# Two non-local attention blocks on one core: chunks of 512 pixels, keys spread over four batches, and the weights W prepared in steps

## The chip, the cores and the metric

The kernel runs on one core of one Trainium2 chip. Its engines are named as in the profile: PE (TensorE, matrix multiplication), DVE (VectorE), ACT (ScalarE), POOL (GpSimd) and SP (SyncE, which here starts most DMAs). The metric is the device time of one execution in microseconds (us). The profile shows one execution of its own. Its span, from the first to the last instruction, is a little shorter than its device time.

## What is computed

Two layers of the same form are applied in turn to `x` of shape (4, 128, 96, 96) in float32: four images of 9216 pixels with 128 channels. One layer, cut to what matters:

```python
g_x = maxpool2(conv1x1(x, g_w, g_b))          # 64 channels, 48 x 48 keys
theta_x = conv1x1(x, theta_w, theta_b)        # 64 channels, 9216 queries
phi_x = maxpool2(conv1x1(x, phi_w, phi_b))    # 64 channels, 48 x 48 keys
attn = softmax(theta_x^T phi_x)               # 9216 x 2304 for each image
y = attn g_x
W_y = conv1x1(y, W_w, W_b), then batch norm with stored mean and variance
return W_y + x
```

The pooling takes the largest of every 2 x 2 pixels, so one image has 2304 keys, in 18 tiles of 128. The order of the keys is free, as long as phi and g have the same.

## The kernel before, in words

**Blocks.** A block is one layer of one image. `ORDER` lists the eight blocks so that a block's predecessor in the same image lies at least one block back. The keys of a block are made while the block ahead of it is at work; only the first block's keys have to be made at the start. After the main program, `general_blocks` would be run if a check of the sums of exponentials failed. That code is not touched.

**Pairs and batches.** A pair is 1024 pixels (two tiles of 512); a block has nine, the program 72. For each pair the 18 key tiles are taken two at a time in nine batches, 648 in all, counted by `t` in one long loop. In each batch PE makes the scores of two key tiles (`scores`, L312), ACT takes their exponential with a constant shift in place of the maximum (L318), DVE adds the results up (`add_up`, L325 and L327), and PE multiplies the batch before by the values (`values`, L335). A matmul uses a 64 x 64 quarter of the array, and four run side by side. Each float32 matmul stands in the trace as two instructions.

**Cycles and slots.** Eighteen batches, two pairs, are a cycle. The slot `s` is the place in it. The other work is put into slots by hand:

- the two thetas for a later pair (`thetas`, slots 5 and 6),
- the sums of the two pairs that are done (`denominators`, slot 3, from the tile `folded`),
- `inverses`, `normalise`, and the projection with W (`multiply`, then `add`, slots 8 and 11),
- the chunks for the next block's keys (`chunks`, slots from `CHUNK_SLOTS` = 1, 13, 15, 17, the first half in one batch and the second half in the next).

All of these use the two PSUM banks of the pool `ps_misc`. Scores have two double banks of their own (`ps_sc`), and the exponentials have seven buffers (`EXPS`).

**The order of the queues is that of the program text.** In a batch it is: scores of the first tile, the `first` piece of other work, scores of the second tile, the `second` piece; then DVE's adds with `take` (the reading of the banks) after the first of them; then the values of the batch before; then the small DVE work, and last the spreads and the list `after`. Each engine executes its own part of this in order.

**Keys.** A chunk is 384 pixels, four rows of the image. PE makes g (partitions 0 to 63) and phi (64 to 127), DVE takes the maximum of 2 x 2 (`pool`, L224) into `gphi`. There are 24 chunks in a block, two at a time. When eight chunks are there (six key tiles), two batches later `spread` does in one go: for the first six tiles the centre, the mean of phi over them (L251, L252); phi less the centre on ACT (L253) and its copy to the other 64 partitions (L256); and eight DVE transposes of g, 32 x 192 each (L264), into `gT`.

**The first block.** It has spreads of three tiles (`FIRST_GT`). Eight chunks and two spreads come ahead of batch 0, and four chunks each in batches 0, 1, 3 and 4 (`between`), with the spreads named in `after`.

**W.** `make_scale`, `make_W` (a PE transpose at L109 and two DVE copies) and `make_shift` (a matmul with W at L161 and DVE work) run one right after another: for layer 0 after batch 7, for layer 1 after batch 18.

Of the kernel before, what the change touches and what calls it, by code (L numbers as in the profile page):

```python
# [9 lines left out]
F32 = mybir.dt.float32  # L10
# [6 lines left out]
P = 128  # L17
B, C, CI, H, W = 4, 128, 64, 96, 96
HW = H * W
# [16 lines left out]
NB = NKT // KB  # L36
EXPS = 7
FIRST_GT = 3
WARM = (5, 3)
CYCLE = 2 * NB  # L40
CHUNK_SLOTS = (1, 13, 15, 17)
# [6 lines left out]
def shifted_blocks(ctx: ExitStack, tc: tile.TileContext, x: bass.AP, layers, out: bass.AP, flag):  # L48
# [58 lines left out]
    def transposed(src, rows, cols, name, twice=False):  # L107
        ps = ps_misc.tile([P, QT], F32, tag="misc", name=f"{name}_ps")
        nc.tensor.transpose(ps[:cols, :rows], src, ident[:rows, :rows])  # L109
        t = const.tile([2 * cols if twice else cols, rows], F32, name=name)  # L110
        nc.vector.tensor_copy(t[:cols, :], ps[:cols, :rows])
        if twice:
            nc.vector.tensor_copy(t[cols:, :], ps[:cols, :rows])
        return t
# [58 lines left out]
    def columns(wanted, name, engine):  # L173

        rows = prep.tile([len(wanted), C], F32, name=f"rows_{name}")
        for i, (w, key) in enumerate(wanted):
            n = w.p[key].shape[0]
            for h in range(C // n):
                engine.dma_start(out=rows[i : i + 1, ts(h, n)], in_=as_row(w.p[key]))

        def make():
            cols = transposed(rows, len(wanted), C, f"cols_{name}")
            for i, (w, key) in enumerate(wanted):
                w.col[key] = cols[:, i : i + 1]

        return make
# [15 lines left out]
    class Block:  # L202
# [5 lines left out]
        def begin_keys(self, gt):  # L208
            name, self.gt = self.name, gt
            self.gphi = kvp.tile([P, NK], F32, tag="gphi", name=f"gphi_{name}", bufs=1)  # L210
            self.phi = kvp.tile([P, NK], F32, tag="phi", name=f"phi_{name}")
            self.gT = kvp.tile([P, NKT, CI], F32, tag="gT", name=f"gT_{name}")
            self.centre = kvp.tile([P, 1], F32, tag="centre", name=f"centre_{name}")

        def products(self, r, ps):

            for h in range(2):
                nc.tensor.matmul(
                    ps[ts(h, CI), :CC], lhsT=self.w.gphi[:, ts(h, CI)],
                    rhs=self.xt[:, ts(r, CC)], start=True, stop=True,  # L220
                )

        def pool(self, r, ps):
            nc.vector.tensor_reduce(  # L224
                self.gphi[:, ts(r, CC // 4)].rearrange("p (h w) -> p h w", w=W // 2),
                ps[:, :CC].rearrange("p (h a w b) -> p h w a b", a=2, b=2, w=W // 2),
                AX.XY,
                ALU.max,
            )

        def pooled(self, r):

            ps = ps_misc.tile([P, QT], F32, tag="misc", name=f"gphi_ps_{self.name}_{r}")
            self.products(r, ps)
            self.pool(r, ps)

        def pooled_2(self, r):

            ps = ps_sc.tile([P, PT], F32, tag="sc", name=f"gphi_ps_{self.name}_{r}")
            for step in (self.products, self.pool):  # L240
                for c in range(2):
                    step(r + c, ps[:, ts(c, QT)])

        def spread_phi(self, i):

            gphi, phi, centre, n = self.gphi, self.phi, self.centre, self.gt * KT
            keys = ts(i, n)
            if i == 0:  # L250
                nc.vector.tensor_reduce(centre[CI:, :], gphi[CI:, keys], AX.X, ALU.add)  # L251
                nc.vector.tensor_scalar(centre[CI:, :], centre[CI:, :], -1.0 / n, None, ALU.mult)  # L252
            nc.scalar.activation(  # L253
                phi[CI:, keys], gphi[CI:, keys], AF.Identity, bias=centre[CI:, :]
            )
            nc.scalar.copy(phi[:CI, keys], phi[CI:, keys])  # L256

        def spread_g(self, i):

            tiles = ts(i, self.gt)  # L260
            g = self.gphi[:CI, :].rearrange("p (t k) -> p t k", k=KT)
            for k in range(KT // 32):
                for c in range(CI // 32):
                    nc.vector.transpose(  # L264
                        self.gT[ts(k, 32), tiles, ts(c, 32)], g[ts(c, 32), tiles, ts(k, 32)]
                    )

        def spread(self, i):
            self.spread_phi(i)
            self.spread_g(i)  # L270

        def chunks(self, r):

            pss = two_banks(f"gphi_ps_{self.name}_{r}")

            def part(i, rows, c):
                return (
                    pss[i][ts(c, CI), :CC], self.w.gphi[rows, ts(c, CI)],
                    self.xt[rows, ts(r + i, CC)],
                )  # L280

            def take():
                for i in range(2):
                    self.pool(r + i, pss[i])

            return crosswise(part, take)

# [206 lines left out]
    def begin(n, gt=GT):  # L494

        blocks[n].xt = xs[ORDER[n][0]]
        blocks[n].begin_keys(gt)
# [12 lines left out]
    begin(0, FIRST_GT)  # L510
# [6 lines left out]
    b0.pooled(1)  # L517
    first_cols()
    for w in ws:
        w.make_std()  # L520
    nc.scalar.preload_act_table(AF.Exp)
    b0.pooled_2(2)
    th = ps_sc.tile([P, PT], F32, tag="sc", name="theta_ps_0")[:, :QT]
    pairs[0].theta(th)
    pairs[0].take_theta(th)
    b0.spread_phi(0)
    b0.pooled(4)
    b0.pooled(5)
    b0.pooled_2(6)
    b0.spread_phi(1)  # L530
    b0.spread_g(0)
    xs[1] = load_x(1)
    between = {0: 8, 1: 12, 3: 16, 4: 20}
    after = {
        0: [lambda: b0.spread_g(1)],
        1: [lambda: b0.spread_phi(2), lambda: b0.spread_g(2)],
        2: [lambda: b0.spread_phi(3), lambda: b0.spread_g(3)],
        4: [lambda: b0.spread_phi(4), lambda: b0.spread_g(4)],
        5: [lambda: b0.spread_phi(5), lambda: b0.spread_g(5)],
        6: [other_cols, ws[0].make_scale, ws[1].make_scale],  # L540
        7: [ws[0].make_W, ws[0].make_shift],
        NB: [ws[1].make_gphi, ws[1].make_theta],
        2 * NB: [ws[1].make_W, ws[1].make_shift],
# [3 lines left out]
    for n in range(1, len(blocks)):  # L547
        lo = (n - 1) * NP * NB if n > 1 else CYCLE
        slots = [t for t in range(lo, n * NP * NB - 4) if t % CYCLE in CHUNK_SLOTS]
        items = HW // CC // 2  # L550
        for i in range(items):
            keys[slots[i * (len(slots) - 1) // (items - 1)]] = (n, i)
# [3 lines left out]
    for t in range(total + 1):  # L556
# [4 lines left out]
        if t in keys:  # L561
            n, i = keys[t]
            if i == 0:
                begin(n)
            first, *pending = blocks[n].chunks(2 * i)
            if i % 4 == 3:
                spreads[t + 2] = lambda n=n, i=i: blocks[n].spread(i // 4)
        elif t < total and s == 5:
            if q < late:
                first, *pending = thetas(pairs[q + 1 : q + 3])  # L570
            else:
                ps = ps_misc.tile([P, QT], F32, tag="misc", name="theta_ps_last")
                first, take = (lambda: odd.theta(ps)), (lambda: odd.take_theta(ps))
        elif gone and s == 3:
            second, take = denominators(gone, folded)
        elif gone and s in (8, 11):
            second, take = gone[s // 11].multiply, gone[s // 11].add
# [15 lines left out]
        if second:  # L593
            second()
        for i in range(KB):
# [4 lines left out]
        if t in between:  # L600
            b0.pooled(between[t])
            b0.pooled(between[t] + 1)
            b0.pooled_2(between[t] + 2)
        if gone and s in (9, 12):
            gone[s // 12].note(gone[s // 12].rc)
# [4 lines left out]
        if t < total:  # L610
            if gone:
                one, two = gone
                if s == 1:
                    two.fold(folded)
                    two.add_halves()
                if s in (4, 5):
                    one.inverses(one.rc, ((0, 1), (2, 3))[s - 4])
                if s == 6:
                    one.normalise()
                if s in (6, 7, 8):  # L620
                    two.inverses(two.rc, ((0,), (1, 2), (3,))[s - 6])
                if s == 9:
                    two.normalise()
            if s == 10:
                even.add_halves()
            if s == 12 and q < late:
                even.fold(folded)
            if q == late:
                if s == 10:
# [3 lines left out]
                    even.inverses(even.rc)  # L633
                if s == 13:
                    even.note(even.rc)
                    even.normalise()
                if s == 15:
# [7 lines left out]
        if t in spreads:  # L645
            spreads.pop(t)()
        for step in after.pop(t, []):
            step()
    assert not spreads and not after
# [322 lines left out]
```

## Time and profile before

| what | us |
|---|---|
| device time, median of 3 runs | 2556.34 (2555.39 to 2557.2) |
| device time of the profiled execution | 2556.96 |
| its span | 2554.8 |
| PE busy in the span | 2523.5 (99%) |
| DVE busy | 2144.2 (84%) |
| ACT busy | 1627.2 (64%) |
| DMA, 59.92 MB | 23 GB/s in the mean |
| start of batch 0, first scores | 12.62 |

Such a page is read as follows. A row of instructions has the line in the kernel, the engine, the operation, what is written from what, the shape and the count; behind the first bar the busy time and the mean duration of one in ns; behind the second bar how long the engine was idle just ahead of such instructions, and whose end let it go on. Busy time of PE counts matmuls that overlap, so 99% does not say how fast they follow each other. In a line of the timeline stand the start in us, the time covered, the engine, the line and the operation, with the count of merged instructions and, in brackets, the idle time ahead of it and what ended it. A line of the waits has the engine and what waited, what it waited for, and then the total in us, how often, and the longest. The granted clock is the share of TensorE's full clock that the profile shows, 0.998 over the whole span.

### The profile page before, as it was taken

What the parts mean: (1) busy time and instruction counts of PE and PEld (TensorE: products, weight loads), DVE (VectorE), ACT (ScalarE), POOL (GpSimd) and SP (SyncE); (2) the same over time, 40 slices, a digit from 0 to 9 for tenths busy, and PEclk for the clock granted to TensorE, in tenths of its full rate; (3) what the DMA queues carried; (4) which work ended last, traced back from release to release, by engine and by line L of the source; (5) the groups of instructions that cost most, each with busy time, mean ns of one, the idle gap of its engine ahead of it and who ended that gap; (6) DMA issues with size and microseconds to landing.
All of it is one profiled execution on the core that took longest, in us unless ns stands there. A gap on an engine that the chain in (4) does not pass through costs nothing.

```text
span 2554.8 us, 54104 instructions
## 1 busy us (share of the span) xinstructions
PE 2523.5 (99%) x23650; PEld 1128.0 (44%) x23650; DVE 2144.2 (84%) x2330; ACT 1627.2 (64%) x1786; POOL 0.7 (0%) x6
## 2 busy tenths in 40 slices
PE   9999999999999999999999999999999999999998
PEld 3333566346653333334665333333466533333332
DVE  7778888888888888888888888888888888888888
ACT  5656666666666666666666666666666666666665
POOL 0000000000000000000000000000000000000000
PEclk9999999999999999999999999999999999999999
DMA  4020000000000000020000000000000000000000
GB/s 153 10 83 10 10 5 10 10 9 10 6 9 26 26 26 26 14 83 9 10 10 5 26 26 26 26 18 8 7 10 10 18 26 14 26 26 26 26 26 35
DMA packets 16586, 59.92 MB, mean 23 GB/s; under 512 B 2635, under 2 KB 3541, under 8 KB 16341
## 3 DMA queue, kind: packets, MB, share of 16 engines
q1 hardware_dynamic: 16172, 56.31, 7.2%
q8 instruction: 187, 3.06, 0.5%
q14 instruction: 59, 0.48, 0.1%
q10 hardware_dynamic: 168, 0.07, 0.0%
HBM read 19.14 MB, written 18.87 MB: 15 GB/s over the span
## 4 chain that ended last, share of the span: by engine, by line


## 5 line engine op out<-in xcount | busy, mean ns | idle before, releaser
L318 ACT ACTIVATE exp<-sc,nshift 128x1024 f32<-128x1024 f32 x1296 | 1387.4, 1112 | 850.8 <-PE sc L312 844.4
L327 DVE TENSOR_TENSOR sum<-sum,exp 128x1024 f32<-128x1024 f32 x1151 | 1399.1, 1216 | 332.8 <-ACT exp L318 287.7
L312 PE MATMUL sc<-theta,phi 64*64 64x512 f32 x10368 | 1308.6, 590 | 11.6 <-ACT exp L318 8.4
L335 PE MATMUL av<-exp,gT 64*64 64x512 f32 x10368 | 1275.9, 589 | 0.0
L312 PEld LDWEIGHTS sc<-theta,phi 64*64 64x64 f32 x10368 | 494.0, 133 | 619.3 <-issue 452.4
L335 PEld LDWEIGHTS av<-exp,gT 64*64 64x64 f32 x10368 | 494.0, 133 | 602.5 <-issue 475.3
L355 DVE RECIPROCAL halves<-halves 128x128 f32<-128x128 f32 x280 | 250.8, 927 | 0.0
L198 PE MATMUL gphi_ps<-x,gphiT 64*64 64x384 f32 x1344 | 148.8, 482 | 0.0
L224 DVE TENSOR_REDUCE gphi<-gphi_ps 128x96 f32<-128x384 f32 x192 | 97.4, 550 | 26.6 <-PE gphi_ps L198 23.8
L325 DVE TENSOR_TENSOR sum<-exp,exp 128x1024 f32<-128x1024 f32 x72 | 87.5, 1215 | 32.3 <-ACT exp L318 29.8
L198 PEld LDWEIGHTS gphi_ps<-x,gphiT 64*64 64x64 f32 x1344 | 66.0, 133 | 78.2 <-issue 55.9
L394 DVE SCALAR_TENSOR_TENSOR x<-W_ps,shift,x 128x512 f32<-128x512 f32 x142 | 99.4, 742 | 0.0
L342 ACT COPY halves<-av 128x1024 f32<-128x1024 f32 x71 | 71.9, 1012 | 27.3 <-PE av L335 26.2
L368 DVE TENSOR_TENSOR folded<-folded,sum 64x1024 f32<-64x1024 f32 x70 | 85.1, 1216 | 1.1
L198 PE MATMUL theta_ps<-x,thetaT 64*64 64x512 f32 x560 | 79.2, 589 | 0.0
L385 PE MATMUL W_ps<-halves,WT 64*64 64x512 f32 x568 | 79.1, 589 | 0.0
L264 DVE STREAM_TRANSPOSE gT<-gphi 32x192 f32<-32x192 f32 (+1 forms) x216 | 74.7, 346 | 2.8
L376 DVE TENSOR_TENSOR halves<-halves 128x512 f32<-128x512 f32 x71 | 48.9, 688 | 0.7
L379 DVE TENSOR_TENSOR halves<-halves 128x512 f32<-128x512 f32 x70 | 47.9, 684 | 0.0
L445 PE MATMUL den_ps<-folded,ones 64*64 64x512 f32 x280 | 40.3, 592 | 6.5 <-DVE gphi L224 6.5
L359 ACT ACTIVATE halves<-den_ps 128x512 f32<-128x512 f32 x70 | 41.1, 600 | 7.5 <-PE den_ps L445 7.5
L372 ACT ACTIVATE halves<-halves 128x512 f32<-128x512 f32 x70 | 44.0, 628 | 0.0
(89 smaller groups left out, 265.3 us busy)
## 6 DMA issues: line engine op xcount, KB each, us to landing
folded<-sum SPq DMA_DIRECT2D x70, 256.0 KB
out_dram<-x SPq DMA_DIRECT2D x35, 512.0 KB
x<-in_x_dram SPq DMA_DIRECT2D x18, 768.0 KB
x<-in_x_dram SPq DMA_DIRECT2D x12, 384.0 KB
out_dram<-x SPq DMA_DIRECT2D x4, 128.0 KB
gphi_nat<-in_L_conv_phi_w_dram SPq DMA_DIRECT2D x2, 32.0 KB
rows_other<-in_L_conv_g_b_dram SPq DMA_DIRECT2D x4, 0.2 KB
W_nat<-in_L_conv_W_w_dram SPq DMA_DIRECT2D x2, 32.0 KB
```

Source lines behind the costliest of these rows:

```text
L198: nc.tensor.matmul(out, lhsT=lhsT, rhs=rhs, start=step == 0, stop=step == 1)
L224: nc.vector.tensor_reduce(self.gphi[:, ts(r, CC // 4)].rearrange("p (h w) -> p h w", w=W // 2), ps[:, :CC].rearrange("p (h a w b) -> p h w ...
L264: nc.vector.transpose(self.gT[ts(k, 32), tiles, ts(c, 32)], g[ts(c, 32), tiles, ts(k, 32)])
L312: nc.tensor.matmul(ps[ts(c, CI), ts(h, QT)], lhsT=self.blk.phi[ts(h, CI), ts(2 * k + c, CI)], rhs=self.th[ts(h, CI), :], start=True, stop= ...
L318: nc.scalar.activation(e, ps, AF.Exp, bias=nshift)
L325: nc.vector.tensor_add(self.sum, self.es[0], e)
L327: nc.vector.tensor_add(self.sum, self.sum, e)
L335: nc.tensor.matmul(self.av[ts(h, CI), ts(r, QT)], lhsT=self.blk.gT[ts(r, CI), k, :], rhs=e[ts(r, CI), ts(h, QT)], start=(k == 0), stop=(k ...
L355: nc.vector.reciprocal(self.rc[:, ts(i, P)], src[:, ts(i, P)])
L368: nc.vector.tensor_add(folded[here, :], folded[here, :], self.sum[here, :])
L385: nc.tensor.matmul(self.pss[h][ts(c, CI), :], lhsT=self.blk.w.W[ts(h, CI), ts(c, CI)], rhs=self.y[ts(h, CI), :], start=True, stop=True,)
L394: nc.vector.scalar_tensor_tensor(dst, self.pss[h], self.blk.w.shift, dst, op0=ALU.add, op1=ALU.add)
```

## The change

- A chunk is 512 pixels and gives exactly one tile of 128 keys. A 96-pixel row does not divide so; a chunk is 8 rows of the left 64 columns, or 16 rows of the right 32. A block has 18 chunks, two at a time, nine items. The moving operand of these matmuls is no longer one contiguous stretch but 8 or 16 of them.
- The items stand at batches 15, 17 and 31 of a double cycle of 36, counted on by one cycle (`KEYS`): slots 13, 15 and 17. Slot 1 has none any more.
- The sums move from slot 3 to 2, the second projection from 11 to 12, and the odd pair's `fold` ahead of the batch's adds in slot 1. Inverses come one in each batch, halves of both pairs are added in slot 1.
- A spread of six tiles takes four batches: centre (first spread only), phi and two transposes in the first; the copy of phi and two transposes in the second; two transposes in each of the other two.
- The first block: four chunks ahead of batch 0, then two in each of the batches 0 to 6, two batches ahead of their use by the scores; phi is made for two tiles at a time, the transposes for six tiles in batches 0, 3 and 6. The centre is the mean over two tiles.
- `make_scale`, `make_W`, `make_shift` and the remaining weights for layer 1 come in the batches 10 to 13, a step in each.

The core of the diff:

```diff
+KEYS = (15, 17, 31)
+THETAS, SUMS, PROJECT = 5, 2, (8, 12)
-FIRST_GT = 3
-CHUNK_SLOTS = (1, 13, 15, 17)
...
+        def chunk(self, k, rows):
+            first, height, left, width = ((0, 8, 0, 64), (8, 8, 0, 64), (0, 16, 64, 32))[k % 3]
+            first += k // 3 * 16
+            pixels = self.xt[rows, :].rearrange("p (h w) -> p h w", w=W)
+            return pixels[:, first : first + height, left : left + width]
...
+        def centring(self, n):
+            centre, gphi = self.centre, self.gphi
+            nc.vector.tensor_reduce(centre[CI:, :], gphi[CI:, : n * KT], AX.X, ALU.add)
+            nc.vector.tensor_scalar(
+                centre[CI:, :], centre[CI:, :], -1.0 / (n * KT), None, ALU.mult
+            )
+
+        def centred(self, keys):
+            nc.scalar.activation(
+                self.phi[CI:, keys], self.gphi[CI:, keys], AF.Identity, bias=self.centre[CI:, :]
+            )
+
+        def copied(self, keys):
+            nc.scalar.copy(self.phi[:CI, keys], self.phi[CI:, keys])
+
+        def square(self, i, k):
+            tiles = ts(i, GT)
+            g = self.gphi[:CI, :].rearrange("p (t k) -> p t k", k=KT)
+            for c in range(CI // 32):
+                nc.vector.transpose(
+                    self.gT[ts(k, 32), tiles, ts(c, 32)], g[ts(c, 32), tiles, ts(k, 32)]
+                )
...
+    pairs[0].theta(th)
+    b0.centring(KB)
+    b0.centred(ts(0, KB * KT))
+    b0.copied(ts(0, KB * KT))
+    pairs[0].take_theta(th)
     for w in ws:
         w.make_std()
     nc.scalar.preload_act_table(AF.Exp)
+    b0.pooled(1)
+    b0.centred(ts(1, KB * KT))
+    b0.copied(ts(1, KB * KT))
...
     after = {
+        10: [other_cols, ws[0].make_scale, ws[1].make_gphi, ws[1].make_scale],
+        11: [ws[0].make_W, ws[1].make_W],
+        12: [ws[0].make_shift, ws[1].make_shift],
+        13: [ws[1].make_theta],
     }
...
     for n in range(1, len(blocks)):
+        cycle = (n - 1) * NP * NB // CYCLE * CYCLE
+        for j in range(NB):
+            t = cycle + KEYS[j % len(KEYS)] + j // len(KEYS) * CYCLE
+            keys[t] = (n, j)
+            if j % len(KEYS) == len(KEYS) - 1:
+                spreads[t + 2] = (blocks[n], j // len(KEYS))
...
+        if gone and s == 1:
+            gone[1].fold(folded)
+        if t + 2 < NB:
+            b0.pooled(t + 2)
         for i in range(KB):
             if t < total:
                 pairs[now].add_up(j * KB + i)
             if i == 0 and take:
                 take()
+        if t + 2 < NB:
+            b0.centred(ts(t + 2, KB * KT))
+            b0.copied(ts(t + 2, KB * KT))
+            if t % 3 == 0:
+                for k in range(KT // 32):
+                    b0.square(t // 3, k)
...
+            for i, pair in enumerate(gone):
                 if s == 1:
+                    pair.add_halves()
+                k = s - PROJECT[i] + 5
+                if k in range(QT // P):
+                    pair.inverses(pair.rc, (k,))
+                if k == QT // P - 1:
+                    pair.normalise()
+            if s == 13 and q < late:
                 even.fold(folded)
...
+        for k in range(KT // 32):
+            if t - k in spreads:
+                blk, i = spreads[t - k]
+                if k == 0:
+                    if i == 0:
+                        blk.centring(GT)
+                    blk.centred(ts(i, GT * KT))
+                if k == 1:
+                    blk.copied(ts(i, GT * KT))
+                blk.square(i, k)
```

More of the change, by code (lines that the diff above doesn't have):

```diff
@@ L105, in as_row, with transposed @@
         return src.rearrange("(o c) -> o c", o=1)
-    def transposed(src, rows, cols, name, twice=False):
-        ps = ps_misc.tile([P, QT], F32, tag="misc", name=f"{name}_ps")
+    def transposed(src, rows, cols, name, twice=False, ps=None):
+        if ps is None:
+            ps = ps_misc.tile([P, QT], F32, tag="misc", name=f"{name}_ps")
         nc.tensor.transpose(ps[:cols, :rows], src, ident[:rows, :rows])
@@ L179, in columns, with make @@
                 engine.dma_start(out=rows[i : i + 1, ts(h, n)], in_=as_row(w.p[key]))
-        def make():
-            cols = transposed(rows, len(wanted), C, f"cols_{name}")
+        def make(ps=None):
+            cols = transposed(rows, len(wanted), C, f"cols_{name}", ps=ps)
             for i, (w, key) in enumerate(wanted):
@@ L206, in __init__, with begin_keys @@
             self.xt, self.w, self.store, self.name = xt, w, store, name
-        def begin_keys(self, gt):
-            name, self.gt = self.name, gt
+        def begin_keys(self):
+            name = self.name
             self.gphi = kvp.tile([P, NK], F32, tag="gphi", name=f"gphi_{name}", bufs=1)
@@ L213, in begin_keys, with pool @@
             self.centre = kvp.tile([P, 1], F32, tag="centre", name=f"centre_{name}")
[L215 to L223, printed above, removed]
+        def chunk(self, k, rows):
[3 more added lines that the diff above has]
+            return pixels[:, first : first + height, left : left + width]
+        def pool(self, k, ps):
+            w = self.chunk(k, slice(0, CI)).shape[2] // 2
             nc.vector.tensor_reduce(
-                self.gphi[:, ts(r, CC // 4)].rearrange("p (h w) -> p h w", w=W // 2),
-                ps[:, :CC].rearrange("p (h a w b) -> p h w a b", a=2, b=2, w=W // 2),
+                self.gphi[:, ts(k, KT)].rearrange("p (h w) -> p h w", w=w),
+                ps.rearrange("p (h a w b) -> p h w a b", a=2, b=2, w=w),
                 AX.XY,
@@ L229, in pool @@
             )
[L231 to L240, printed above, removed]
-                for c in range(2):
[L242 to L265, printed above, removed]
-                    )
[L268 to L274, printed above, removed]
+        def pooled(self, j):
+            pss = two_banks(f"gphi_ps_{self.name}_{j}")
+            for i in range(2):
+                rhs = self.chunk(j * KB + i, slice(0, P))
+                for c in range(2):
+                    nc.tensor.matmul(
+                        pss[i][ts(c, CI), :], lhsT=self.w.gphi[:, ts(c, CI)], rhs=rhs,
+                        start=True, stop=True,
+                    )
+            for i in range(2):
+                self.pool(j * KB + i, pss[i])
@@ L276, in part, with chunks @@
+        def chunks(self, j):
+            pss = two_banks(f"gphi_ps_{self.name}_{j}")
             def part(i, rows, c):
                 return (
-                    pss[i][ts(c, CI), :CC], self.w.gphi[rows, ts(c, CI)],
-                    self.xt[rows, ts(r + i, CC)],
+                    pss[i][ts(c, CI), :], self.w.gphi[rows, ts(c, CI)],
+                    self.chunk(j * KB + i, rows),
                 )
@@ L283, in take @@
                 for i in range(2):
-                    self.pool(r + i, pss[i])
+                    self.pool(j * KB + i, pss[i])
             return crosswise(part, take)
+        def centring(self, n):
[17 more added lines that the diff above has]
+                )
     class Pair:
@@ L492, in shifted_blocks, with begin @@
         blocks.append(Block(None, ws[l], store, f"{b}_{l}"))
-    def begin(n, gt=GT):
+    def begin(n):
         blocks[n].xt = xs[ORDER[n][0]]
-        blocks[n].begin_keys(gt)
+        blocks[n].begin_keys()
     pairs = [Pair(blk, p, n * NP + p) for n, blk in enumerate(blocks) for p in range(NP)]
@@ L507, in busy @@
             nc.tensor.matmul(warm[:, :P], lhsT=ident, rhs=ident, start=True, stop=True)
-    begin(0, FIRST_GT)
+    begin(0)
     b0 = blocks[0]
@@ L516, in shifted_blocks @@
     b0.pooled(0)
-    b0.pooled(1)
-    first_cols()
+    first_cols(ps_sc.tile([P, PT], F32, tag="sc", name="cols_first_ps")[:, :QT])
+    th = ps_sc.tile([P, PT], F32, tag="sc", name="theta_ps_0")[:, :QT]
+    pairs[0].theta(th)
[3 more added lines that the diff above has]
+    pairs[0].take_theta(th)
     for w in ws:
@@ L521, in shifted_blocks @@
     nc.scalar.preload_act_table(AF.Exp)
[L522 to L531, printed above, removed]
+    b0.pooled(1)
+    b0.centred(ts(1, KB * KT))
+    b0.copied(ts(1, KB * KT))
     xs[1] = load_x(1)
-    between = {0: 8, 1: 12, 3: 16, 4: 20}
     after = {
[L535 to L543, printed above, removed]
+        10: [other_cols, ws[0].make_scale, ws[1].make_gphi, ws[1].make_scale],
+        11: [ws[0].make_W, ws[1].make_W],
+        12: [ws[0].make_shift, ws[1].make_shift],
+        13: [ws[1].make_theta],
     }
@@ L547, in shifted_blocks @@
     for n in range(1, len(blocks)):
[L548 to L552, printed above, removed]
+        cycle = (n - 1) * NP * NB // CYCLE * CYCLE
[4 more added lines that the diff above has]
+                spreads[t + 2] = (blocks[n], j // len(KEYS))
     loads = {4 * NB + 4: 2, 31 * NB + 4: 3}
@@ L564, in shifted_blocks @@
                 begin(n)
[L565 to L568, printed above, removed]
+            first, *pending = blocks[n].chunks(i)
+        elif t < total and s == (THETAS if q else THETAS + 2):
             if q < late:
@@ L573, in shifted_blocks @@
                 first, take = (lambda: odd.theta(ps)), (lambda: odd.take_theta(ps))
-        elif gone and s == 3:
+        elif gone and s == SUMS:
             second, take = denominators(gone, folded)
-        elif gone and s in (8, 11):
-            second, take = gone[s // 11].multiply, gone[s // 11].add
+        elif gone and s in PROJECT:
+            pair = gone[PROJECT.index(s)]
+            second, take = pair.multiply, pair.add
         if t < total:
@@ L599, in shifted_blocks @@
                 take()
[L600 to L605, printed above, removed]
+        if t + 2 < NB:
[4 more added lines that the diff above has]
+                    b0.square(t // 3, k)
+        if gone and s in (PROJECT[0] - 1, PROJECT[1] - 1):
+            pair = gone[s // (PROJECT[1] - 1)]
+            pair.note(pair.rc)
         if t:
@@ L610, in shifted_blocks @@
         if t < total:
-            if gone:
-                one, two = gone
+            for i, pair in enumerate(gone):
                 if s == 1:
[L614 to L626, printed above, removed]
+                    pair.add_halves()
[5 more added lines that the diff above has]
+            if s == 13 and q < late:
                 even.fold(folded)
@@ L633, in shifted_blocks @@
                     even.inverses(even.rc)
+                    even.add_halves()
                 if s == 13:
@@ L636, in shifted_blocks @@
                     even.normalise()
-                if s == 15:
+                if s == 16:
                     even.multiply()
@@ L644, in shifted_blocks @@
             pairs[-1].inverses(den)
-        if t in spreads:
-            spreads.pop(t)()
+        for k in range(KT // 32):
[8 more added lines that the diff above has]
+                blk.square(i, k)
         for step in after.pop(t, []):
             step()
-    assert not spreads and not after
+    assert not after
     good = const.tile([P, 2], F32, name="good")
```

## The prediction

> **What bounds the kernel now.** I read the page first, then the waits, then the timeline around each longest wait.
>
> ```profile
> PE 2523.5 (99%) x23650; PEld 1128.0 (44%) x23650; DVE 2144.2 (84%) x2330; ACT 1627.2 (64%) x1786; POOL 0.7 (0%) x6
> ...
> L312 PE MATMUL sc<-theta,phi 64*64 64x512 f32 x10368 | 1308.6, 590 | 11.6 <-ACT exp L318 8.4
> L335 PE MATMUL av<-exp,gT 64*64 64x512 f32 x10368 | 1275.9, 589 | 0.0
> ...
> L198 PE MATMUL gphi_ps<-x,gphiT 64*64 64x384 f32 x1344 | 148.8, 482 | 0.0
> ```
>
> TensorE is the bound, but its busy time cannot say how tightly: the matmuls overlap. The timeline gives pitches. An undisturbed batch (two scores tiles, two values tiles, eight 512-wide instructions each) takes 3.43 us, so eight take 0.858 us; eight 384-wide chunk instructions take 0.645. The counts times these give 1296 x 0.858 x 2 = 2224 for scores and values, 168 x 0.645 = 108 for chunks, 60 for theta, 61 for W, 30 for sums, 15.5 for the first block's chunks: 2499 of 2554.8 us. Only about 56 us can be won at all, and start and end hold much of it. The stops between are in the waits (total, times, longest):
>
> ```profile
> ACT phi L253 <- DVE centre L252: 16.8, 8, 4.4
> ...
> PE sc L312 <- ACT exp L318: 8.4, 7, 2.8
> ...
> PE den_ps L445 <- DVE gphi L224: 6.5, 4, 1.6
> ...
> PE sc L312 <- DVE gphi L224: 3.2, 3, 1.6
> ...
> PE shift_ps L161 <- DVE WT L111: 2.1, 2, 1.2
> ```
>
> Seven stops at exp: one per block made ahead. Four at the sums, two at W. The timeline of the first exp stop:
>
> ```profile
> 176.37 0.95 DVE L251 TENSOR_REDUCE centre<-gphi 64x1 f32<-64x768 f32 x1
> 177.35 0.15 DVE L252 TENSOR_SCALAR centre<-centre 64x1 f32<-64x1 f32 x1
> 177.53 3.04 DVE L264 STREAM_TRANSPOSE gT<-gphi 32x192 f32<-32x192 f32 x8
> 177.53 0.93 ACT L253 ACTIVATE phi<-gphi,centre 64x768 f32<-64x768 f32 x1 [4.38 <-DVE centre L252]
> 178.50 0.83 ACT L256 COPY phi<-phi 64x768 f32<-64x768 f32 x1
> 179.35 2.12 ACT L318 ACTIVATE exp<-sc,nshift 128x1024 f32<-128x1024 f32 x2
> 180.52 3.63 PE L312 MATMUL sc<-theta,phi 64*64 64x512 f32 x16 [2.76 <-ACT exp L318]
> ```
>
> ScalarE stands at phi until VectorE has the centre, then makes phi twice, and the exps behind it come late. And the windows of that stop (PEclk is the third number from the end, before DMA share and GB/s):
>
> ```profile
> 182.00:183.00 1.00, 1.00 (x8) 0.25 (x4) 1.00 (x3) 0.43 (x1) 0.00 (x0) 0.50 0.00 0
> ...
> 185.00:187.00 2.00, 2.00 (x26) 0.59 (x20) 1.45 (x2) 1.49 (x5) 0.00 (x0) 1.00 0.00 0
> ```
>
> After 2.76 us idle the clock ran at half until about 183.8, so this stop cost 4.7 us. The other six cost 1.0 to 1.4 each by the matmuls' starts against their pitch: 12.1 in all. A sums stop:
>
> ```profile
> 255.28 1.23 DVE L327 TENSOR_TENSOR sum<-sum,exp 128x1024 f32<-128x1024 f32 x1
> 256.42 1.01 DVE L224 TENSOR_REDUCE gphi<-gphi_ps 128x96 f32<-128x384 f32 x2
> 257.03 1.12 PE L445 MATMUL den_ps<-folded,ones 64*64 64x512 f32 x5 [1.63 <-DVE gphi L224]
> ```
>
> The sums' two banks are still held by chunks that VectorE could not pool behind transposes and fold. The first bank comes 1.80 late, the second 0.47 later: 2.27, four times, **9.1 us**.
>
> **The change, part by part.**
>
> Chunks of 512. Per block made ahead TensorE has 24 x 4 x 2 = 192 instructions at a pitch of 0.645/8 = 80.6 ns before, and 144 at 107.3 after: 15.48 against 15.45 us, **-0.2 us** for seven blocks. The Trainium skill ("TensorE: Matmul & The Clock Gate", section Measured speedup vs the span model) lets four packed matmuls take one duration plus about 4 ns a tile; with the rows' durations, 48 fours at 482 + 12 would become 36 at 590 + 12, 2.0 us less a block and 14 in all. The trace's fours start 429 ns apart although each lasts 589, so successive fours overlap and I take the pitch. The moving operand now has 8 or 16 broken pieces, which no matmul row shows. Below: nothing, as the same elements stream. Above, one column's time (429/512 = 0.84 ns) per piece, 10.7 pieces on average, 9 ns a four: 252 fours, +2.3 us. I take 0, by the contiguous row. VectorE's pool is 0.51 for 384 columns; at one per 1.04 ns (the 768- against 384-wide reduce, 949 - 551 ns) 512 cost 0.64: 18 x 0.64 against 24 x 0.51, nothing on the path.
>
> Sums at 2, keys only at 13, 15, 17. The last pool before the sums now runs in batch 0, two batches ahead. There VectorE's order is two pools (ending 4.1 us after the batch starts), one add (5.3), at most one transpose step (6.1), fold (7.3); the sums matmuls come at 9.4. All four stops go: **-9.1 us**. The fold moves ahead of two adds, with those queued behind it: its DMA, issued after the last add of batch 17, ends in 2.5 us typically and VectorE comes to it 3.4 to 5 us later. If it came late, the exps have seven buffers, so adds some microseconds late stop nobody.
>
> Keys spread in steps. Transposes in four steps of two (0.74 each instead of 3.04), phi and its copy a batch apart. The second and third spread of a block then fit: phi starts when the last exp of batch 15 ends and takes 0.93, before the next scores are there. **The first spread does not.** Centring still sits behind that batch's last add. From the end of that exp, 3.94 us after batch 15 begins: add 1.26, centre and scale 1.17, phi 0.96, exp 1.1, add 1.26, two pools of the chunk at 15 1.28, signal 0.05: 11.0. The chunk at 17 needs those banks at 2 x 4.29 + 0.86 = 9.44 (these batches carry half a chunk pair each). So **TensorE stops 1.6 us there, seven times: 11.1 us** in place of 12.1: **-1.0**. What is gained is mainly the half clock. Bounds: 0, if the centre came before the last add; 2.5 each if the transpose step got in too.
>
> W at 12, chunk at 13. Adds of W (2 x 0.74) end at about 5.0 after batch 12 starts, the banks are wanted at 5.15: nothing, but with 0.1 us to spare; up to 0.5 each of 21 places if not, 0 to +10. The output's DMA of the odd pair goes a batch later, past no other on SP but the move at 0, two batches away. Inverses one a batch keep VectorE at 3.4 of 3.43 us; the normalised tile is ready over a batch ahead of its multiply. The even pair's halves are added in batch 1, just ahead of the sums' copies, which may wait 0.6 us on ScalarE with 0.9 to spare. At the end W moves from 15 to 16; its adds finish at 2537.5, before the last sum at 2537.9: 0.
>
> W prepared in steps. Each transpose is copied a whole batch before its use. The two stops (1.5 and 1.2 us late) and the restarts after them (0.17 each) go: **-3.0**. Transposes themselves stay.
>
> The first block. Before, scores start at 12.62 with eight chunks (3072 pixels) done. After, walked with the rows: pools to 8.5, columns, centre 9.3, phi and copy to 10.25, theta 10.95, scores at 11.0 with 2048 pixels; but then the exp table (1.28) and the second phi stand ahead of the first exp, 13.7. Batches 0 to 6 hold 5.15 us of TensorE work each, and eight transposes (3.04) stand on VectorE behind pools and adds in batches 0, 3, 6. Values then wait 1.7, 1.4 and 2.2 us in batches 1, 4 and 7. Batch 9 comes at 59.8; before it is 61.6 with about 2.5 us of W work in it: **+0.9** after equal work. Here a rule weighs: the same page (section HAM oscillation) has the clock fall only after idle gaps of about 3.4 us, by which 2.2 costs nothing more. The trace differs: 2.76 idle halved it for some 3.3 us, losing 1.7, while 1.61 at 20.35 did not. 2.2 lies between; I take no drop, with +1.7 kept above.
>
> **Sum**: -0.2 - 9.1 - 1.0 - 3.0 + 0.9 = -12.4. From the profiled execution's 2556.96 (span 2554.8 and 2.2 around it) to 2544.6; the median of the runs is 0.6 lower, so **2544**, 0.5% faster.
>
> **Rivals.** (a) The first spread does not stop either and the head is no worse: 11.1 and 0.9 more, **2532**. For it: six of the seven stops before were about 1 us, so little slack would do; against: the chain above has no gap to squeeze. (b) New small waits eat it: 0.3 us at 21 places after W, 1.7 of half clock in the head: 2544 + 8 = **2552**. The thin 0.1 us speaks for it; a chunk pair already follows another within two batches without a PE stop on most cycles. (c) **Slower**: the broken moving operand. If each piece costs TensorE ten columns' time instead of none, a four takes 90 ns more; 252 fours give +23, **2566**. It decides from 50 ns a four, 12.4 us in all. For it, no matmul in the trace reads so; against, VectorE's pool reads PSUM in pairs at full pace.
>
> **Numbers.** Forecast 0.52, (a) 0.19, (b) 0.15, (c) 0.14. This kernel's runs tell 0.2% (5 us) from nothing. Faster by more: forecast, (a) and half of (b): 0.78; same 0.09; slower 0.13. Range 2531 to 2554: it holds (a) and (b) and leaves (c) out.
>
> **What would show it.** den_ps gone from the waits on gphi; shift_ps gone; seven waits of gphi_ps (L198's successor) on DVE gphi, about 1.5 us each, in the second batch after each centre; batch 9 near 60 us; the pitch of eight chunk matmuls at 0.86. A pitch of 0.95 or more makes it wrong on the slow side, and no wait behind the centre on the fast side.

## The result and the profile after

The changed kernel takes 2544.43 us (median of 4 runs, 2544.34 to 2544.58) against 2556.77 us for the kernel before beside it (4 runs, 2555.39 to 2558.14). The ratio is 0.9952, with an interval of 0.9935 to 0.9969. The span fell from 2554.8 to 2542.5 us. The forecast was 2544.

The page of the changed kernel; line numbers moved by one or more (scores L313, values L336, chunks and thetas L199, pools L225):

```profile
PE 2525.2 (99%) x23290; PEld 1380.7 (54%) x23290; DVE 2170.6 (85%) x2258; ACT 1625.2 (64%) x1792; POOL 0.7 (0%) x6
...
L313 PE MATMUL sc<-theta,phi 64*64 64x512 f32 x10368 | 1470.0, 589 | 0.3 <-ACT theta L307 0.3
L336 PE MATMUL av<-exp,gT 64*64 64x512 f32 x10368 | 1424.7, 589 | 1.0 <-DVE gT L285 1.0
...
L199 PE MATMUL gphi_ps<-x,gphiT 64*64 64x512 f32 x1008 | 171.3, 591 | 5.1 <-DVE gphi L225 5.1
```

PE's busy time rose by 1.7 us while the kernel became 12 us shorter. Busy time of overlapping matmuls says nothing here; the idle times behind the second bar do. Scores stood for 11.6 us before, 8.4 of them behind exp; now it is 0.3. What is new stands in the last row: 5.1 us in which chunks wait for DVE's pools. The waits:

```profile
ACT phi L272 <- DVE centre L267: 21.7, 8, 4.7
...
PE gphi_ps L199 <- DVE gphi L225: 5.1, 7, 0.7
```

The waits of `den_ps` for `gphi` and of `shift_ps` for W are gone. The wait for the centre is not: it became longer (16.8 before). Seven chunks wait, one for each block made ahead. The timeline around the first of them, PE with its weight loads (PEld), DVE and ACT (start, time covered, idle time ahead in brackets):

```profile
157.72 1.11 ACT L319 ACTIVATE exp<-sc,nshift 128x1024 f32<-128x1024 f32 x1 [0.60 <-PE sc L313]
158.86 1.23 DVE L328 TENSOR_TENSOR sum<-sum,exp 128x1024 f32<-128x1024 f32 x1 [0.49 <-ACT exp L319]
...
160.10 0.95 DVE L266 TENSOR_REDUCE centre<-gphi 64x1 f32<-64x768 f32 x1
...
161.08 0.15 DVE L267 TENSOR_SCALAR centre<-centre 64x1 f32<-64x1 f32 x1
...
161.27 0.93 ACT L272 ACTIVATE phi<-gphi,centre 64x768 f32<-64x768 f32 x1 [2.44 <-DVE centre L267]
...
162.23 2.12 ACT L319 ACTIVATE exp<-sc,nshift 128x1024 f32<-128x1024 f32 x2
163.37 1.22 DVE L328 TENSOR_TENSOR sum<-sum,exp 128x1024 f32<-128x1024 f32 x1 [1.36 <-ACT exp L319]
...
164.51 1.28 DVE L225 TENSOR_REDUCE gphi<-gphi_ps 128x128 f32<-128x512 f32 x2
...
165.25 1.25 PE L199 MATMUL gphi_ps<-x,gphiT 64*64 64x512 f32 x5 [0.74 <-DVE gphi L225]
...
165.85 0.14 PEld L199 LDWEIGHTS gphi_ps<-x,gphiT 64*64 64x64 f32 x3 [0.41 <-DVE gphi L225]
```

The lines down to the pools are a chain, each starting where the one above ends: add, centre, phi, exp, add, pools. From the end of the exp at 158.83 to the end of the pools at 165.79 it is 6.96 us; the prediction added up 7.03 without the signal.

The bracket shows 0.74 us of idle time, but PE loses more. The scores ahead of the chunk start at 163.48, so by the pitch the chunk would start at 164.34. The matmul of its first quarter needs only the bank that the first pool frees, and starts at 165.25. The next in the queue writes the other bank, so it and the two behind it wait for the second pool: three of the four quarters start at 165.85 (the last line), 1.5 late. The scores behind them keep this distance. Against run 5 below, in which nothing waits at this place, three quarters lose 1.55 us at each of the seven stops.

### The profile page after: what moved, and what is told of

It is laid out like the page before. It is cut to its first block, busy times and chain, and to the rows that moved or that the text cites. A ratio compares the mean times of both kernels' runs of the same rounds, so it can differ in the third digit from the quotient of the medians.

```text
span 2542.5 us, 53323 instructions
## 1 busy us (share of the span) xinstructions
PE 2525.2 (99%) x23290; PEld 1380.7 (54%) x23290; DVE 2170.6 (85%) x2258; ACT 1625.2 (64%) x1792; POOL 0.7 (0%) x6
## 4 chain that ended last, share of the span: by engine, by line
PE 97%; DVE 2%; ACT 1%; issue 0%; POOL 0%; DVEq 0%; POOLq 0%
PE sc L313 43%; PE av L336 43%; PE gphi_ps L199 4%; PE W_ps L386 2%; PE theta_ps L199 2%; PE den_ps L446 1%; DVE sum L328 1%; ACT exp L319 1%; PE gphi_ps L238 0%; ACT phi L272 0%; DVE centre L266 0%; DVE gT L285 0%; DVE gphi L225 0%; PE warm_ps L508 0%; DVE sum L356 0%
## 5 line engine op out<-in xcount | busy, mean ns | idle before, releaser
L313 PE MATMUL sc<-theta,phi 64*64 64x512 f32 x10368 | 1470.0, 589 | 0.3 <-ACT theta L307 0.3
L336 PE MATMUL av<-exp,gT 64*64 64x512 f32 x10368 | 1424.7, 589 | 1.0 <-DVE gT L285 1.0
L313 PEld LDWEIGHTS sc<-theta,phi 64*64 64x64 f32 x10368 | 641.3, 133 | 496.4 <-issue 476.2
L336 PEld LDWEIGHTS av<-exp,gT 64*64 64x64 f32 x10368 | 628.9, 133 | 506.9 <-issue 470.2
L199 PE MATMUL gphi_ps<-x,gphiT 64*64 64x512 f32 x1008 | 171.3, 591 | 5.1 <-DVE gphi L225 5.1
L225 DVE TENSOR_REDUCE gphi<-gphi_ps 128x128 f32<-128x512 f32 x144 | 93.2, 684 | 39.4 <-PE gphi_ps L199 28.8
L199 PE MATMUL theta_ps<-x,thetaT 64*64 64x512 f32 x560 | 94.4, 589 | 0.0
L199 PEld LDWEIGHTS gphi_ps<-x,gphiT 64*64 64x64 f32 x1008 | 62.2, 132 | 59.1 <-issue 34.1
L285 DVE STREAM_TRANSPOSE gT<-gphi 32x192 f32<-32x192 f32 x192 | 70.7, 368 | 3.6
L386 PEld LDWEIGHTS W_ps<-halves,WT 64*64 64x64 f32 x568 | 36.2, 133 | 27.0 <-issue 27.0
L199 PEld LDWEIGHTS theta_ps<-x,thetaT 64*64 64x64 f32 x560 | 35.6, 133 | 27.2 <-issue 26.9
```

The lines of the kernel that those rows point to most:

```text
L199: nc.tensor.matmul(out, lhsT=lhsT, rhs=rhs, start=step == 0, stop=step == 1)
L225: nc.vector.tensor_reduce(self.gphi[:, ts(k, KT)].rearrange("p (h w) -> p h w", w=w), ps.rearrange("p (h a w b) -> p h w a b", a=2, b=2, w=w),
L313: nc.tensor.matmul(ps[ts(c, CI), ts(h, QT)], lhsT=self.blk.phi[ts(h, CI), ts(2 * k + c, CI)], rhs=self.th[ts(h, CI), :], start=True, stop= ...
L336: nc.tensor.matmul(self.av[ts(h, CI), ts(r, QT)], lhsT=self.blk.gT[ts(r, CI), k, :], rhs=e[ts(r, CI), ts(h, QT)], start=(k == 0), stop=(k ...
L386: nc.tensor.matmul(self.pss[h][ts(c, CI), :], lhsT=self.blk.w.W[ts(h, CI), ts(c, CI)], rhs=self.y[ts(h, CI), :], start=True, stop=True,)
```

## The experiments

All are variants of the changed kernel, but for one of the kernel before. Times are medians. The first four ran beside the kernel before at 2556.33, the last four beside 2556.16, and the changed kernel beside 2556.77, so differences to the changed kernel are good to about 0.6 us.

**1. Every spread in one batch again, the slots as changed.**

```diff
-        for k in range(KT // 32):
-            if t - k in spreads:
-                blk, i = spreads[t - k]
...
+        if t in spreads:
+            blk, i = spreads[t]
+            if i == 0:
+                blk.centring(GT)
+            blk.centred(ts(i, GT * KT))
+            blk.copied(ts(i, GT * KT))
+            for k in range(KT // 32):
                 blk.square(i, k)
```

> The changed kernel with each spread again in one batch (phi, its copy and eight transposes at slot 15), all slots as changed. Steps account: the first spread's chain to the banks of the chunk at 17 grows by the six transposes more (2.3 us) and the copy: stop about 2.5 us instead of 1.8, and the second spread now stops too, 1.4 us; +16 us in all, about 2560. Slots account (the stops went because slot 1 is free and the sums come early): no more than 2 us, 2544 to 2546. Fewer-instructions account (144 chunk matmuls a block instead of 192 make the gain): 2544.

Measured: 2561.04 us, ratio to the kernel before 1.0021 (1.0012 to 1.0031). Its waits:

```profile
PE gphi_ps L199 <- DVE gphi L225: 9.2, 14, 0.9
...
PE sc L313 <- ACT exp L319: 4.1, 7, 0.6
```

Fourteen chunk waits, two in each block, where there were seven, and seven waits for exp. With the new slots but without the steps the kernel is slower than the one before. The sums do not stop in it, but the burst of phi, copy and eight transposes now stops the chunk at slot 17.

**2. Chunks at slot 1 and sums at slot 3 again, with steps.**

```diff
-KEYS = (15, 17, 31)
-THETAS, SUMS, PROJECT = 5, 2, (8, 12)
+KEYS = (15, 17, 19, 31, 33, 35, 37, 49, 51)
+THETAS, SUMS, PROJECT = 5, 3, (8, 12)
...
-            t = cycle + KEYS[j % len(KEYS)] + j // len(KEYS) * CYCLE
+            t = cycle + KEYS[j]
...
```

> The changed kernel with chunks at slot 1 again (items at 15, 17, 19, 31, 33, 35, 37, 49, 51 of the double cycle) and the sums at slot 3, spreads in steps. Steps account: the sums find their banks free (pools end 13.7 us after slot 0 starts, sums want them at 14.6), no wait of den_ps; the first spread moves to slot 3, where an inverse stands ahead of the centre, and stops the scores about 1.9 us, seven times, in place of today's 1.8 at the chunk: 2543 to 2547. Slots account: the sums' stops come back, 2.3 us at seven second spreads, +16, about 2560.

Measured: 2546.21 us, ratio 0.9963 (0.9949 to 0.9977). No `den_ps` waits for `gphi`. In place of the chunk's wait there are seven of the scores at the first spread:

```profile
PE sc L313 <- ACT exp L319: 7.5, 7, 1.1
```

**3. The same with every spread in one batch** (the edits of 1 and 2 together).

> As the one before, but each spread in one batch. Both accounts: sums' stops at the second spreads (slot 1), 1.4 to 2.3 us each, and scores' stops at the first spreads of 2.8 us idle, with the half clock up to 4.5: 2563 to 2580. The difference from the run with steps is what the steps are worth in the old slots: 16 to 36 us by the steps account, under 15 by the slots account, as the sums would stop in both.

Measured: 2563.92 us, ratio 1.0033 (1.0018 to 1.0047). Its waits:

```profile
PE sc L313 <- ACT exp L319: 13.5, 7, 1.9
...
PE den_ps L446 <- DVE gphi L225: 5.5, 7, 0.8
```

The stops at the sums are back. Between this and run 2 only the steps differ: 17.7 us, near the low end of what was expected. The scores' stop had 1.9 us idle where 2.8 was expected, and in the profile three of the seven were followed by the half clock (last section).

**4. The kernel before with steps, and nothing else of the change.** `spread` gets the step `k`: phi (and the centre) at 0, the copy at 1, two transposes in each.

```diff
...
-        if t in spreads:
-            spreads.pop(t)()
+        for k in range(KT // 32):
+            if t - k in spreads:
+                blk, i = spreads[t - k]
+                blk.spread(i, k)
...
```

> The kernel before with one part of the change: its spreads in four steps over four batches, chunks of 384, slots and W as before. Steps account: den_ps no longer waits for gphi (-9), and the scores' stops at the first spreads shrink by the copy's 0.83 us to 0 to 0.4 each, 2 us for the longest (-9): about 2539, below the changed kernel. Slots account: den_ps still waits, 2550 or more. Fewer-instructions account: 2556.

Measured: 2540.7 us, ratio 0.9942 (0.9925 to 0.9959). This one part is worth more than the whole change: its four runs (2540.06 to 2541.85) all lie below those of the changed kernel. The timeline of the sums where the kernel before stopped, at batch 57 (pools L224, sums' matmuls L461):

```profile
250.03 0.74 DVE L284 STREAM_TRANSPOSE gT<-gphi 32x192 f32<-32x192 f32 x2
...
250.80 1.23 DVE L343 TENSOR_TENSOR sum<-sum,exp 128x1024 f32<-128x1024 f32 x1
...
251.94 1.02 DVE L224 TENSOR_REDUCE gphi<-gphi_ps 128x96 f32<-128x384 f32 x2
...
252.87 1.22 PE L461 MATMUL den_ps<-folded,ones 64*64 64x512 f32 x8
```

Only two transposes (0.74) stand ahead of the add and the pools where there were eight (3.04). The first pool ends near 252.4 and the second is over about when the sums' matmuls on its bank begin; no idle bracket stands at them. The scores' waits at the first spreads shrank from 8.4 us in seven to

```profile
PE sc L328 <- ACT exp L334: 2.5, 4, 1.9
```

since the copy of phi (0.83) no longer stands ahead of the exps. In the old slots no chunk was due two batches behind the centre; the new ones put one there in every block. That is where the whole change lost part of what its steps had gained; the table behind run 5 has the amounts.

**5. The centre one batch earlier.**

```diff
+        if t + 1 in spreads and spreads[t + 1][1] == 0:
+            spreads[t + 1][0].centring(GT)
         for k in range(KT // 32):
...
                 if k == 0:
-                    if i == 0:
-                        blk.centring(GT)
                     blk.centred(ts(i, GT * KT))
```

> The changed kernel with the centre of a block made one batch earlier (end of slot 14, behind that batch's adds), phi still at slot 15. If the chain of the prediction (last add, centre, phi, exp, add, pools) makes the stop at the chunk of slot 17, it goes: seven times 1.8 us, 2532, no wait of gphi_ps on DVE gphi. If the pools and transposes alone hold the banks, it stays within 1 us of 2544.

Measured: 2533.5 us, ratio 0.9911 (0.9894 to 0.9927), 10.9 us under the changed kernel. The same place of the timeline:

```profile
156.32 0.95 DVE L266 TENSOR_REDUCE centre<-gphi 64x1 f32<-64x768 f32 x1
...
157.30 0.15 DVE L267 TENSOR_SCALAR centre<-centre 64x1 f32<-64x1 f32 x1
...
158.68 0.93 ACT L272 ACTIVATE phi<-gphi,centre 64x768 f32<-64x768 f32 x1
...
162.46 1.28 DVE L225 TENSOR_REDUCE gphi<-gphi_ps 128x128 f32<-128x512 f32 x2
...
164.15 1.04 PE L199 MATMUL gphi_ps<-x,gphiT 64*64 64x512 f32 x8
```

The centre now lies in a gap that DVE had, phi follows the exp without a wait, the pools end 0.4 us ahead of the chunk, and no bracket stands at it. No chunk waits in the whole run. The chain through the centre was the cause; 1.8 us a stop was expected, and it is 1.56 (10.9 / 7).

In this run PE stops nowhere between the start of batch 19 and that of batch 647, so it tells what the others lose there. The times are from the starts of the scores in each trace. By batch 19 the changed kernel and the runs 2 and 5 have two chunk pairs behind them that the others still have ahead; their 3.43 us are added here:

| kernel | batch 19 to 647, us | over run 5 |
|---|---|---|
| before | 2437.57 | 21.5 |
| run 2 | 2429.06 | 13.0 |
| changed | 2426.88 | 10.9 |
| run 4 | 2422.23 | 6.2 |
| run 5 | 2416.02 | 0 |

For the kernel before, the prediction had 12.1 for the first spreads and 9.1 for the sums, 21.2 together. Steps in the old slots leave 6.2 of this, steps in the new ones 10.9. Run 2 warns against laying the difference on slot 1 alone: its chunks stand there too, but close behind one another, and it loses more than the changed kernel.

**6. The first block's transposes ahead of the adds.**

```diff
             b0.pooled(t + 2)
+            if t % 3 == 0:
+                for k in range(KT // 32):
+                    b0.square(t // 3, k)
         for i in range(KB):
...
             b0.copied(ts(t + 2, KB * KT))
-            if t % 3 == 0:
-                for k in range(KT // 32):
-                    b0.square(t // 3, k)
```

> The changed kernel, first block only: in batches 0, 3 and 6 the eight transposes come ahead of the batch's adds on DVE. If the values of batches 1, 4 and 7 wait for transposes that stand behind adds, the three waits of 1.3, 0.8 and 2.0 us go: about 2540. If the adds then come too late for somebody, no gain: 2544 or more.

Measured: 2540.31 us, ratio 0.9937 (0.992 to 0.9953), 4.1 us under the changed kernel. No values wait for `gT` any more. The adds come later, and PE waits for none of them.

**7. W and shift of a layer in one batch.**

```diff
-        11: [ws[0].make_W, ws[1].make_W],
-        12: [ws[0].make_shift, ws[1].make_shift],
+        11: [ws[0].make_W, ws[0].make_shift],
+        12: [ws[1].make_W, ws[1].make_shift],
```

> The changed kernel with W and shift of a layer in one batch again (11 and 12). The prediction's step: the matmul for the shift waits for DVE's copies of W, 1.5 and 1.2 us and restarts: +3, 2547. If something else hides it: 2544.5.

Measured: 2547.04 us, ratio 0.9964 (0.995 to 0.9978), 2.6 us over the changed kernel. In its timeline:

```profile
71.16 0.30 PE L110 MATMUL WT_ps<-ident,W_bn 128*64 128x128 f32 x1
72.34 0.28 DVE L112 COPY WT<-WT_ps 64x128 f32<-64x128 f32 x1
...
72.67 0.38 PE L162 MATMUL shift_ps<-cols_other,WT 64*128 64x1 f32 x2 [1.21 <-DVE WT L112]
```

The copy is queued on DVE behind the batch's adds and comes 0.9 us after the transpose is done. PE stands until then, with all scores of the next batch behind it.

**8. Runs 5 and 6 together.**

> The changed kernel with the early centre and the transposes first. If the two stops are separate, their gains add up: 12.5 + 4, about 2528. If one stop only uncovers the next, less than the larger of the two.

Measured: 2529.12 us, ratio to the kernel before 0.9895 (0.9878 to 0.9911). The gains of 10.9 and 4.1 add up to 15.0, and together they are 15.3: the stops are separate, and removing one uncovered no other. This version beats both kernels.

## Why the prediction was right

The path that it gave holds: the stops at the sums go, a new one comes at the chunk behind the centre, and W stops no more. The first block it had less well.

- **Chunks, -0.2.** Right. In the changed kernel's timeline eight chunk matmuls start at 155.75 and the scores after them at 156.61: 0.86 us for eight 512-wide instructions, the pitch of contiguous ones. The broken operand costs nothing that can be seen, so rival (c) falls. The 14 us that the prediction estimated for fewer fours, and did not take, fall too: runs 1 and 3 have the same few chunk instructions and are slower than the kernel before.
- **Sums, -9.1.** The amount is right: the four stops are gone. The reason was only half of it. The prediction put it under the new slots, and run 1, with these and no steps, has no stop at the sums; but it stops twice a block at the chunks instead. Runs 2 and 4 have no stop at the sums with slot 1 in use and sums at 3, and run 3 has it without steps. Either is enough at the sums; only the steps shorten the burst itself.
- **First spread, 12.1 to 11.1.** Right in place, count and size: seven chunk stops at slot 17, 1.6 us forecast for each and 1.55 measured, and run 5 gains 10.9 us by removing them. Rival (a), no stop, falls by the seven waits.
- **W at 12 with a chunk at 13: 0.** Right with its 0.1 us to spare. All chunk waits of the changed kernel are the seven behind a centre; rival (b) falls.
- **W in steps, -3.0.** Run 7 measures 2.6.
- **First block, +0.9.** The mechanism was right and the size a little off. Values waited in batches 1, 4 and 7, late by 1.3, 0.8 and 2.0 us where 1.7, 1.4 and 2.2 were forecast, and run 6 gains 4.1 by removing this. Still batch 9 came at 60.47, not 59.8. Scores began at 11.45 rather than 11.0, and this is chance: in the seven runs whose code ahead of batch 0 is the same (all but run 4) they began anywhere from 10.41 to 11.38. The first eight chunk matmuls took 2.69 us here and 1.94 in run 7, with fours starting 0.91 and 0.75 apart where the later pitch is 0.43, as at half the clock. The clock's entries in this trace begin only at 7.13, so that cause is not shown. After equal work in batch 19 (100.82 less 3.4 for the two chunk pairs, against 98.12) head and W together gained 0.7 rather than 2.1; with W at 2.6, the head cost 1.9.
- **The rest.** About as much came back where the sum had nothing. Batch 19 to 647 gained 10.7 us against 10.3 forecast (0.2, 9.1 and 1.0), and the end 0.9 against 0: from the start of the last scores it took 19.13 before and 18.27 after. Of this, 0.74 lies in the last 16 matmuls with W, 1.83 us before and 1.09 after. Before, the clock fell to half at 2545.98, in their midst, and after at 2536.40, behind them. Run 4, with the end of the kernel before, has 1.09 too, so this is chance and no gain of the change.
- **Half clock in the head.** The clock did not fall in batches 0 to 9; the longest idle time ahead of values was 0.48 us in one piece, since the two halves of their matmuls came free one after another. The half clock of the first stop before (batch 39) went with that stop.

That the total came within 1 us of the forecast is partly luck: the head was about 1 us off one way and W 0.4 the same way, while the clock at the end gave back 0.7 by chance and the batches between 0.4. No run separates the head from its chance of about 1 us.

## What to carry to other kernels

Where one engine is the bound at 99%, look for the instructions that stand behind a wait in a strict queue of another engine: here a 1.1 us mean over keys, behind an add and ahead of the exps, cost 11 us in seven stops, and moving it one batch earlier won all of it. Walk such a chain end to end with durations from the trace and compare it with when the result is wanted; the walk found stops that the engines' busy shares (DVE 84 and 85%) did not show. Splitting a burst into steps was worth 16 us alone, and the new places of the chunks gave part of it back, so try each part of a change by itself. Compare starts of the same batch between two traces: they show where a gain arises, and that 1 us at either end can be chance.

## What the runs showed of the hardware that was not expected

The clock of PE can fall to half after short stops, and not each time. In run 3 the scores stopped at the first spreads with 1.92 to 1.93 us idle, seven times. Windows behind such stops, some of only 0.1 us (PEclk is the third number from the end):

```profile
401.80:405.00 3.20, 3.20 (x32) 1.26 (x36) 3.06 (x4) 2.39 (x3) 0.00 (x0) 1.00 0.02 5
752.00:752.10 0.10, 0.10 (x8) 0.08 (x4) 0.10 (x1) 0.10 (x1) 0.00 (x0) 0.75 0.00 0
752.40:755.00 2.60, 2.60 (x16) 0.80 (x12) 2.50 (x4) 1.11 (x1) 0.00 (x0) 0.50 0.03 6
755.40:755.50 0.10, 0.10 (x8) 0.08 (x4) 0.10 (x1) 0.00 (x0) 0.00 (x0) 0.69 0.00 0
1386.90:1387.00 0.10, 0.10 (x8) 0.10 (x4) 0.10 (x1) 0.10 (x1) 0.00 (x0) 0.65 0.00 0
2021.80:2021.90 0.10, 0.10 (x7) 0.03 (x3) 0.10 (x1) 0.10 (x1) 0.00 (x0) 0.54 0.00 0
2554.20:2554.30 0.10, 0.10 (x8) 0.08 (x4) 0.07 (x2) 0.04 (x1) 0.00 (x0) 0.94 0.00 0
```

The stop ahead of 401.80 kept the full clock. A PEclk between 0.5 and 1 tells where in its window the clock changed: 0.75 means in the middle, so it fell at 752.05, and 0.69 that it was back at 755.46. It ran at half for 3.41 us, which is 1.7 us of time. The falls at 1386.93 and 2021.81 follow stops of the same length, and the one at 2554.29 lies at the kernel's end.

These four falls lie 634.88, 634.88 and 532.48 us apart: 186, 186 and 156 steps of 3.4133 us. In the kernel before, the falls at 180.54 and 2545.98 are 693 such steps apart. In all ten traces the changes of the clock lie whole steps apart, so it changes on a grid of 3.41 us that the stops do not shift. The Trainium skill ("TensorE: Matmul & The Clock Gate", section What's actually happening) has this as a free-running window of 3413 ns, and the traces agree.

The grid tells the seven stops of run 3 apart. Those that lost the clock lie whole within one step, as 749.53 to 751.45 in the step from 748.64 to 752.05. The four that kept it lie across a point of the grid, as 399.86 to 401.78 across 400.48. So the idle time alone is no threshold: not the 2.76 us that the prediction took as the nearest row, and not the 3.4 us of the same page (section HAM oscillation), since 1.92 was enough here. Nor is the place a whole rule. A stop of 1.89 us in run 4 (177.68 to 179.56) lies in one step too, 177.10 to 180.52 as counted back from the fall at 2532.30, and kept the clock. What decides there stays open.

The times of run 1 spread most (2559.19 to 2567.87 in ten runs), and it had the most stops. Its granted clock was 0.995 in the slowest run, 0.997 in the next and 0.998 or 0.999 in the others. A drop of 0.004 in 2558 us is about 10 us of clock, near the 8.7 between the slowest and the fastest, so the clock by itself is large enough to make the spread.
